# Counting the softmax sums of three groups once, and four projections in halves, in a two-layer graph attention kernel

## The chip, the cores and the metric

The kernel runs on one core of a Trainium2 chip. The metric is the device time of one execution in microseconds (us); lower is better. The core has five engines that run side by side, each through its own list of instructions in order: TensorE (PE; PEld is its weight load) multiplies matrices, VectorE (DVE) and ScalarE (ACT) work elementwise and may read the matmul results in PSUM, GpSimd (POOL) works elementwise on SBUF and issues one kind of DMA, SyncE (SP) issues the other DMAs. Engines wait for each other by semaphores.

## What is computed

16 images, each with 1024 nodes of 256 features and its own 1024 x 1024 adjacency matrix. Two layers follow each other; each normalizes, applies a relu, and adds masked multi-head attention to its input. Layer 0 has 4 heads of 64 features, layer 1 has 8 heads of 32 and biases on q, k and v.

```python
h = jnp.maximum(_layernorm(x, axis=-1), 0.0)
q, k, v = heads(h @ Wq), heads(h @ Wk), heads(h @ Wv)          # per layer
scores = jnp.einsum('bhnd,bhmd->bhnm', q, k) / math.sqrt(D)
scores = jnp.where(adjacency > 0, scores, -jnp.inf)
w = jax.nn.softmax(scores, axis=-1)
out = jnp.einsum('bhnm,bhmd->bhnd', w, v)
x = x + concat(out) @ Wo + bo
```

All of it is in float32. The softmax is computed without a running maximum: exponentials p, the products p v, and the sums of p over the keys (the "counts"), by which the products are divided at the end.

## The kernel before

**Steps.** The attention of an image in a layer is cut into halves of 512 queries (`qh`), each half into two groups (`g`): in layer 1 a group is 4 heads, in layer 0 it is 2. A step of layer 1 handles one tile of 128 keys for the 4 heads of its group, a step of layer 0 two tiles of keys for 2 heads, so each step makes 4 blocks of 128 keys x 512 queries. A group has 8 steps in layer 1 and 4 in layer 0; an image has 32 and 16. The steps of all images stand in one list: layer 0 of image b+2 follows layer 1 of image b, so that each image's layer 1 is framed by layer 0 of others. In what follows c is the first step of an image's layer 1. Its groups 0 to 3 (`2*qh+g`) start at c, c+8, c+16 and c+24, and layer 0 of another image starts at c+32.

**One step on the engines.** `scores` (L501) makes the 4 blocks in two PSUM pairs; `exponentials` masks them on VectorE (L524, two instructions) and takes the exponential on ScalarE (L530); `weigh` (L542) multiplies by v. `weigh` of a step runs two steps later (`LEAD = 2`). There are three PSUM pairs (`ps_s`, 2 banks each), and two single banks: `po` for the weighed sums and `pz` for the counts. The exponentials of an even step lie in a tile of the ring `p0` (7 buffers), those of an odd step in `p10` and `p11` (2 buffers each), so an odd step writes where the odd step four before it was.

**Counts in layer 1** (`count_steps`, L643 to L690). After an odd step's `weigh`, GpSimd adds the odd step's tile to the even one's (L659, two additions). So a group has four sums of pairs, after j = 1, 3, 5 and 7. An accumulating DMA that GpSimd issues (`accumulate`, L643, 1 MB) adds one of them to another. What is left is summed over the 128 keys by `count` (L387): a matmul with a column of ones into the bank `pz`. In groups 0, 1 and 2 the first two sums are joined and counted, and so are the last two: two counts to a group, given in halves of 256 columns at two steps (`halves`) or whole. In group 3 all four are joined by three DMAs and counted once. Image 14 (`brief`) does group 3 otherwise, and the last image (`pairs`) counts every sum of a pair.

**After a group** (`end_group`). `spread` copies the counts from PSUM and sends them by DMA (L420) into a shape in which `invert` takes the reciprocal (L428) and writes it to DRAM (L430); `fetch` reads it back over all partitions (L439); `normalize` multiplies on GpSimd (L447); `end_half` multiplies by Wo (L483) and adds to x. Each is given a number of steps after the group's end.

**The order around it.** `Stream.run` walks over the steps, two at a time in layer 0. In each it issues scores, the weighs that wait, counts that are due, exponentials, and then all that was put down for the step with `later(i, f)`; functions named in `LARGE` go last. If an even step of layer 1 has a LARGE function, its weighs are put off to the next step. Every engine's instructions run in the order of this program. Projections of coming images (`kq`, L304, and `values`, L345: 8 or 16 instructions, 3.63 us or 3.65 us of TensorE) are LARGE and use a PSUM pair; they are put down, like the layer norms (`stats`, `norm`), the transposes by DMA (`turn_blocks`, `put_blocks`, `place_blocks`) and the loads of masks, at fixed steps from c, or from a, the first step of the layer 0 that follows.

Of the kernel before, what the change touches and what calls it, by code (L numbers as in the profile page):

```python
# [10 lines left out]
F32 = mybir.dt.float32  # L11
# [7 lines left out]
P = 128  # L19
# [5 lines left out]
LARGE = ("k", "q", "values", "end_half")  # L25
# [65 lines left out]
def fast_program(ctx, tc, a, w, loads, chk):  # L91
# [89 lines left out]
    class Inputs:  # L181
# [106 lines left out]

        def kq(self, half, is_q):
            if half == 0 and not is_q:  # L290
                self.kT = actp.tile([P, 2, N], F32, tag="kT", name=f"kT_{self.n}")
                self.v = actp.tile([P, NT, E], F32, tag="v", name=f"v_{self.n}")
# [41 lines left out]

        def k(self, half):
            self.kq(half, False)
# [18 lines left out]
    class Group:  # L355


        def __init__(self, inp, mask, qh, g, half):
# [11 lines left out]
            self.waits = ((5, 5), (7, 7), (7, 6), None)[2 * qh + g]  # L370
# [197 lines left out]
    class Stream:  # L568
# [76 lines left out]
        def count_steps(self, i, st):  # L645
# [7 lines left out]
            elif j % 2:  # L653
                one = self.steps[i - LEAD - 1].p
                if gr.last and not (gr.brief or gr.pairs) and j == 7:
                    self.accumulate(gr.two, gr.one)
# [9 lines left out]
                elif j == 3:  # L666
                    self.accumulate(one, gr.one)
                    gr.one = one
                    if not gr.last:
                        self.halves(i + gr.waits[0], gr, one, True, False)  # L670
                    if gr.brief:
                        self.later(i + 6, gr.count, one, True, False)
                elif gr.brief and j == 5:
                    self.halves(i + 5, gr, one, False, False)
                elif gr.brief:
                    self.later(i + 4, gr.count, one, False, st.last)
                elif j == 5:
                    gr.two = one
                elif not gr.last:
                    self.accumulate(one, gr.two)  # L680
                    if gr.qh:
                        self.later(i + 6, gr.count, one, False, True)
                    else:
                        self.halves(i + gr.waits[1], gr, one, False, True)
                else:
                    self.later(i + 1, self.accumulate, one, gr.two)
                    self.later(i + 4, gr.count, one, True, True)
# [12 lines left out]
        def end_group(self, i, gr):  # L700
# [6 lines left out]
            if gr.layer == 0:  # L707
# [5 lines left out]
                at = (3, 4, 5, 7, 11) if gr.qh else (3, 5, 6, 7, 11)  # L713
                if gr.inp.b == B - 1 and gr.qh:
                    at = 3, 4, 5, 7, 13
                if gr.inp.b == 0:
                    at = (2, 3, 4, 5, 8) if gr.qh else (3, 5, 6, 7, 9)
            else:
                at = ((6, 12, 15, 19), (8, 12, 14, 17, 19), (6, 9, 11, 14), None)[2 * gr.qh + gr.g]
# [428 lines left out]
```

## Time and profile before

| what | value |
| --- | --- |
| median of 3 runs | 3096.69 us (3095.47 to 3098.55) |
| profiled execution | 3095.46 us |
| its span, first to last instruction | 3093.7 us |
| granted TensorE clock | 0.999 |
| L387 counts on TensorE | 1928 instructions, 179.7 us |
| L659 additions on GpSimd | 510 of 2429 ns |
| L643 accumulating DMAs | 133 of 1024 KB, issue 919 ns, median 7.7 us to landing |
| L524 on VectorE | 1536 of 1214 ns, 1792.0 us |
| L530 on ScalarE | 1536 of 1055 ns, 1607.8 us |

An f32 matmul of 512 columns stands in the trace as two instructions; four matmuls of 32 rows or columns run beside each other in the array, so a tile of layer 1 is 8 instructions. A matmul's end is modelled, and durations of neighbours overlap: what one costs is read from its start to the next one's start. In lines of a timeline the columns are start, duration, engine, line of the program, operation, out<-in, shapes and number of instructions, and in brackets how long the engine had been idle and who ended that. "PE po L542" in such a bracket is a guess from the semaphores and may be another.

### The profile page before, as it was taken

Reading aid. Unit: us, or ns where it says so; the run is one execution under the profiler, and the core shown is the slowest. Engines: PE = TensorE matmul, PEld = TensorE weight load, DVE = VectorE, ACT = ScalarE, POOL = GpSimd, SP = SyncE. Lnnn points to the kernel's source line nnn. Section 1 sums busy time; section 2 is a strip of 40 time slices with the busy share of each in tenths; the row PEclk is TensorE's granted clock in tenths of the full one; section 3 lists DMA queues with packets and bytes.
Section 4 is the critical chain, followed back from the end, with each engine's and each line's share of the span. In section 5 each row is a group of like instructions: output and inputs, shape, how many; then the busy total and the mean of one; then the engine's idle time right before and its main releaser. Section 6 shows DMA issues by size and latency. Waiting matters only on the chain.

```text
span 3093.7 us, 47320 instructions
## 1 busy us (share of the span) xinstructions
PE 3072.4 (99%) x17398; PEld 1219.0 (39%) x17398; DVE 2473.7 (80%) x2698; ACT 2230.8 (72%) x2436; POOL 2434.0 (79%) x1554
## 2 busy tenths in 40 slices
PE   9999999999999999999999999999999999999998
PEld 4443433434334343443433434343343433434333
DVE  6678787887878888788887887878788787887777
ACT  5667767777777777777777777777777777776675
POOL 3578788787887878878788787887878788787887
PEclk9999999999999999999999999999999999999999
DMA  4225545354463544535445363554535545453331
GB/s 133 62 66 118 126 110 125 115 113 120 103 143 108 120 122 102 141 103 121 119 100 138 106 129 104 114 130 107 127 114 113 127 110 120 120 113 86 76 77 33
DMA packets 259232, 341.40 MB, mean 110 GB/s; under 512 B 58288, under 2 KB 218288, under 8 KB 241968
## 3 DMA queue, kind: packets, MB, share of 16 engines
q0 software_dynamic: 19152, 139.47, 22.6%
q1 hardware_dynamic: 239520, 198.56, 22.3%
q8 instruction: 139, 2.28, 0.3%
q14 instruction: 101, 0.83, 0.1%
q10 hardware_dynamic: 320, 0.26, 0.0%
HBM read 149.95 MB, written 47.96 MB: 64 GB/s over the span
## 4 chain that ended last, share of the span: by engine, by line
PE 93%; DVE 2%; DMA 1%; SPq 1%; ACT 1%; issue 1%; POOL 0%; DVEq 0%; ACTq 0%; POOLq 0%
PE ps L501 31%; PE po L542 29%; PE pq L304 15%; PE pv L345 7%; PE py L483 7%; PE pz L387 4%; DVE p L524 2%; DMA sums<-s 1%; SPq L152 0%; SPq L420 0%; ACT p L530 0%; POOL p L659 0%; DMA p<-p 0%; DMA inv<-vd 0%; DVE x L488 0%
## 5 line engine op out<-in xcount | busy, mean ns | idle before, releaser
L524 DVE SCALAR_TENSOR_TENSOR p<-mask,ps 128x1024 f32<-128x1024 fp8e5 x1536 | 1792.0, 1214 | 360.5 <-PE ps L501 340.5
L530 ACT ACTIVATE p<-p 128x1024 f32<-128x1024 f32 x1536 | 1607.8, 1055 | 633.3 <-DVE p L524 576.5
L659 POOL TENSOR_TENSOR p<-p,p 128x1024 f32<-128x1024 f32 x510 | 1212.6, 2429 | 163.5 <-PE po L542 163.5
L501 PE MATMUL ps<-qT,kT 32*128 32x512 f32 (+1 forms) x6144 | 1074.3, 629 | 5.0 <-DVE p L524 4.2
L542 PE MATMUL po<-p,v 128*32 128x512 f32 (+1 forms) x6144 | 980.3, 600 | 1.6 <-ACT cat L399 1.3
L501 PEld LDWEIGHTS ps<-qT,kT 32*128 32x128 f32 (+1 forms) x6144 | 348.9, 184 | 590.4 <-issue 239.3
L542 PEld LDWEIGHTS po<-p,v 128*32 128x32 f32 (+1 forms) x6144 | 234.2, 118 | 680.9 <-issue 474.5
L555 POOL TENSOR_TENSOR p<-p 128x1024 f32<-128x1024 f32 x128 | 302.5, 2363 | 92.8 <-DVE p L554 87.5
L554 POOL TENSOR_TENSOR p<-p,p 128x1024 f32<-128x1024 f32 x64 | 150.7, 2355 | 170.1 <-DVE p L551 128.7
L345 PE MATMUL pv<-wv,hT 128*128 128x256 f32 x1024 | 237.8, 385 | 0.1
L304 PE MATMUL pq<-hT,wk 128*128 128x512 f32 x512 | 236.7, 605 | 0.7 <-DVE p L524 0.6
L304 PE MATMUL pq<-hT,wq 128*128 128x512 f32 x512 | 236.8, 605 | 0.1
L483 PE MATMUL py<-wo,cat 128*128 128x256 f32 x1008 | 234.4, 386 | 0.1
L447 POOL TENSOR_TENSOR cat<-cat,inv 128x512 f32<-128x512 f32 x127 | 173.8, 1374 | 76.4 <-DMA inv<-vd 75.8
L345 PEld LDWEIGHTS pv<-wv,hT 128*128 128x128 f32 x1024 | 189.4, 190 | 72.6 <-DVE p L524 22.2
L483 PEld LDWEIGHTS py<-wo,cat 128*128 128x128 f32 x1008 | 186.3, 190 | 74.2 <-issue 27.2
L387 PE MATMUL pz<-p,ones 128*32 128x256 f32 (+1 forms) x1928 | 179.7, 444 | 1.3 <-DMA p<-p 1.3
L551 DVE TENSOR_TENSOR p<-p 128x1024 f32<-128x1024 f32 x128 | 178.5, 1394 | 0.0
L643 POOL DMA_DIRECT2D p<-p x133 | 122.2, 919 | 61.2 <-POOL p L659 30.1
L221 ACT ACTIVATE hn<-x,shift,rstd 128x256 f32<-128x256 f32 x251 | 135.6, 588 | 40.3 <-DMA turned<-hn 26.0
L399 ACT COPY cat<-po 128x512 f32<-128x512 f32 x128 | 73.3, 572 | 118.6 <-PE py L483 96.7
L488 DVE TENSOR_TENSOR x<-py,x 128x1024 f32<-128x1024 f32 x63 | 77.1, 1224 | 101.8 <-PE py L483 101.4
(62 smaller groups left out, 1770.3 us busy)
## 6 DMA issues: line engine op xcount, KB each, us to landing
p<-p POOLq DMA_DIRECT2D x133, 1024.0 KB, 7.7
adj<-in_adj_dram SPq DMA_DIRECT2D x512, 128.0 KB, 3.0
turned<-hn SPq DMA_DIRECT2D x58, 512.0 KB, 3.8
hT<-turned SPq DMA_DIRECT2D x232, 128.0 KB, 2.9
x<-in_x_dram SPq DMA_DIRECT2D x128, 128.0 KB, 3.1
inv<-vd SPq DMA_DIRECT2D x128, 128.0 KB, 3.0
inv<-vd SPq DMA_DIRECT2D x252, 64.0 KB, 3.2
out_dram<-x SPq DMA_DIRECT2D x124, 128.0 KB, 2.2
```

Source lines behind the costliest of these rows:

```text
L304: nc.tensor.matmul(pq[:, m, :], wt[self.layer][:, c, ts(m, P)], self.hT[half][:, c, :], start=(c == 0), stop=(c == 1),)
L345: nc.tensor.matmul(pv[:, i, :], self.hT[half][:, c, ts(i, P)], w.v[self.layer][:, c, :], start=(c == 0), stop=(c == 1),)
L387: nc.tensor.matmul(self.s[ts(r, 32), q], w.ones.to_broadcast([P, 32]), of[:, q], start=start and not part, stop=stop and part != 0,)
L447: nc.gpsimd.tensor_mul(o, o, inv)
L483: nc.tensor.matmul(py[:, i, :], self.half.cat[:, c, ts(i, P)], w.o[self.layer][:, c, :], start=(c == 0), stop=(c == 1),)
L501: nc.tensor.matmul(st.ps[i // 2][:, i % 2, :], gr.inp.kT[r * D : (r + 1) * D, gr.g, ts(kt, P)], gr.inp.qT[gr.qh][r * D : (r + 1) * D, gr.g ...
L524: nc.vector.scalar_tensor_tensor(out=half, in0=gr.mask.m[gr.qh][:, kt // 4, :, kt % 4].unsqueeze(1).to_broadcast([P, 2, 512]), scalar=-EDG ...
L530: nc.scalar.activation(half, half, AF.Exp, scale=gr.scale)
L542: nc.tensor.matmul(gr.o[r * D : (r + 1) * D, :], gr.inp.v[:, kt, h * D : (h + 1) * D], st.halves[i // 2][:, i % 2, :], start=(kt == 0), st ...
L551: nc.vector.tensor_add(a, a, b)
L555: nc.gpsimd.tensor_add(a, a, b)
L659: nc.gpsimd.tensor_add(half, half, of)
```

## The change

Seven things are changed, all in when and how often work is issued; what is computed stays the same.

1. Groups 0, 1 and 2 of layer 1 join all four sums by three DMAs, as group 3 did, and count once: group 0 whole at c+18, group 1 in two halves (c+24, c+25), group 2 whole at c+33, which is layer 0's second step.
2. The second accumulation of a group stands behind the additions of j = 7. The third is put down one step later in groups 1 and 3, two steps later in groups 0 and 2, and in image 14 two steps later in all of 0 to 2.
3. Four projections of the next layer 0 (k of the first half at c+8 and c+10, q of the first half at c+12 and c+16, k of the second half at c+20 and c+22, values of the second half at c+28 and c+30) are made in two parts each, each part in the single bank `pz` in place of a PSUM pair. The parts are LARGE.
4. `spread`, `invert`, `fetch` and `normalize` of groups 0 and 2 move: group 0 from (6, 12, 15, 19) to (9, 11, 13, 19) after its end, group 2 from (6, 9, 11, 14) to (10, 12, 14, 16).
5. In the second half of layer 0 `normalize` moves from 7 to 11 steps after the end and `end_half` from 11 to 13 (steps c+12 and c+14 of the layer 1 that runs then).
6. The layer norms of the image whose layer 1 comes next start earlier: for its first half from a-20, a-16, a-15, a-13 to a-26, a-22, a-19, a-17 (c+6, c+10, c+13, c+15), and the DMA transposes with them.
7. Images 14 and 15 get numbers of their own for some of these.

The core of the diff:

```diff
+        def part(self, half, is_q, m):
...
+            pq = ps_o.tile([P, 512], F32, tag="pz", name=f"pq_{self.n}_{half}_{int(is_q)}_{m}")
+            for c in range(2):
+                nc.tensor.matmul(
+                    pq, wt[self.layer][:, c, ts(m, P)], self.hT[half][:, c, :],
+                    start=(c == 0), stop=(c == 1),
+                )
+            (nc.vector.tensor_copy if is_q else nc.scalar.copy)(to[:, m, :], pq)
...
+        def values_part(self, half, m):
+            pv = ps_o.tile([P, 512], F32, tag="pz", name=f"pv_{self.n}_{half}_{m}")
...
-            self.waits = ((5, 5), (7, 7), (7, 6), None)[2 * qh + g]
+            self.waits = (9, 7, 8, 4)[2 * qh + g]
...
-                if gr.last and not (gr.brief or gr.pairs) and j == 7:
-                    self.accumulate(gr.two, gr.one)
                 for k, of in enumerate(st.halves):
                     half = one[:, ts(k, 2), :]
                     nc.gpsimd.tensor_add(half, half, of)
...
+                elif j == 5:
+                    gr.two = one
+                elif st.last and gr.last:
+                    self.accumulate(gr.two, gr.one)
+                    self.later(i + 1, self.accumulate, one, gr.two)
+                    self.later(i + gr.waits, gr.count, one, True, True)
+                elif st.last:
+                    self.accumulate(gr.two, gr.one)
+                    late = not gr.g or gr.qh or gr.inp.b == B - 2
+                    self.later(i + (2 if late else 1), self.accumulate, one, gr.two)
+                    if gr.g:
+                        self.halves(i + gr.waits, gr, one, True, True)
+                    else:
+                        self.later(i + gr.waits, gr.count, one, True, True)
+                else:
                     self.accumulate(one, gr.one)
                     gr.one = one
...
-                at = (3, 4, 5, 7, 11) if gr.qh else (3, 5, 6, 7, 11)
+                at = (3, 4, 5, 11, 13) if gr.qh else (3, 5, 6, 7, 11)
...
-                at = ((6, 12, 15, 19), (8, 12, 14, 17, 19), (6, 9, 11, 14), None)[2 * gr.qh + gr.g]
+                at = ((9, 11, 13, 19), (8, 12, 14, 17, 19), (10, 12, 14, 16), None)[2 * gr.qh + gr.g]
...
-            norms(mine, 0, a - 20, a - 16, a - 15, a - 13, bias=a)
-            block_inputs(mine, 0, a - 10, a - 8, a - 4, a, a + 2, a + 8)
-            norms(mine, 1, a - 14, a - 10, a - 8, a - 6, bias=a + 6)
+            norms(mine, 0, a - 26, a - 22, a - 19, a - 17, bias=a)
+            block_inputs(mine, 0, a - 14, a - 11, a - 5, a, a + 2, a + 8)
+            norms(mine, 1, a - 14, a - 13, a - 8, a - 6, bias=a + 6)
...
-                block_inputs(other, 0, c, c + 1, c + 2, c + 8, c + 16, c + 18)
+                block_inputs(other, 0, c, c + 1, c + 2, (c + 8, c + 10), (c + 12, c + 16), c + 18)
...
-                block_inputs(other, 1, c + 7, c + 8, c + 12, c + 22, c + 26, c + 30)
+                block_inputs(other, 1, c + 7, c + 8, c + 12, (c + 20, c + 22), c + 26, (c + 28, c + 30))
```

The index i in `count_steps` is the step whose turn it is when the weigh of step c+7 (or c+15, c+23) has been issued, that is two steps after it: i = c+9, c+17, c+25.

## The prediction

> **What bounds the kernel now.** I read the page first (busy shares, chain of waits), then the busy time of the stages of one image, then the timelines of TensorE, of GpSimd and of all engines.
>
> ```profile
> PE 3072.4 (99%) x17398; PEld 1219.0 (39%) x17398; DVE 2473.7 (80%) x2698; ACT 2230.8 (72%) x2436; POOL 2434.0 (79%) x1554
> ...
> PE 93%; DVE 2%; DMA 1%; SPq 1%; ACT 1%; issue 1%; POOL 0%; DVEq 0%; ACTq 0%; POOLq 0%
> ```
>
> TensorE sets the time: 99% busy and 93% of the chain. An average hides stages, so here are the two stages of one image in the middle: 16 steps of layer 0, then 32 steps of layer 1 (columns: PE, PEld, DVE, ACT, POOL, clock, DMA).
>
> ```profile
> 1259.98:1336.74 76.76, 76.62 (x340) 31.34 (x336) 59.24 (x64) 56.28 (x60) 58.99 (x41) 1.00 0.50 124
> 1336.74:1449.86 113.12, 113.08 (x738) 43.34 (x736) 95.67 (x105) 82.72 (x94) 94.39 (x57) 1.00 0.47 113
> ```
>
> TensorE is full in both. In layer 1, where the change lies, VectorE has 95.7 and GpSimd 94.4 of 113.1 us: about 85% each, with little room.
>
> **TensorE's prices**, from start to next start in its timeline:
>
> ```profile
> 1380.29 1.14 PE L501 MATMUL ps<-qT,kT 32*128 32x512 f32 x8
> 1381.36 1.06 PE L542 MATMUL po<-p,v 128*32 128x512 f32 x8
> 1382.24 0.61 PE L387 MATMUL pz<-p,ones 128*32 128x256 f32 x8
> 1382.79 1.15 PE L501 MATMUL ps<-qT,kT 32*128 32x512 f32 x8
> 1383.94 3.72 PE L483 MATMUL py<-wo,cat 128*128 128x256 f32 x16
> 1387.59 1.14 PE L501 MATMUL ps<-qT,kT 32*128 32x512 f32 x8
> 1388.66 1.93 PE L542 MATMUL po<-p,v 128*32 128x512 f32 x16
> 1390.52 1.14 PE L501 MATMUL ps<-qT,kT 32*128 32x512 f32 x8
> ```
>
> Scores of a step 1.07 us (1.15 ahead of a full-array product); weighing 0.88 for one step, 1.86 for two in a run; half a count 0.55 at the end of a run; a full-array product 3.65. So a tile of 512 columns costs 0.885 and the end of a run 0.09; half a count inside a run is 0.445. A whole count alone takes 0.98 (1259.01 to 1259.98).
>
> **What is removed.** c is the first layer-1 step of an image. Group 0 loses two whole counts in halves and gets one whole one, group 1 goes from four halves to two, group 2 from two halves and a whole one to one whole one: three tiles, 3 x 0.885 = 2.66 us an image, in images 0 to 14 (the last image counts in pairs and stays). 15 x 2.66 = 39.9 us. Bounds by the rows: 0.445 to 0.98 for a tile.
>
> **Projections in halves.** A half is four of eight instructions, 3.63/2 = 1.82 us (bounds 1.8 to 1.9). Four more even steps become "large": each costs 0.08 (1.15 for 1.07) and joins two weighs into one run (-0.09). Sum: nothing. Their copies are ACT 0.57 x 2 for 1.0 (L399, L349) and DVE 0.69 x 2 for 1.23 (L310, L313), some 0.15 us more each, under ACT's 27% idle time; each bank is needed again two steps (5 us) later. Without that cover they would cost 0.6 us an image.
>
> **What is added on GpSimd.** Each of groups 0 to 2 gets a third accumulating DMA. The issue takes 0.9 us of GpSimd, three are 2.7 of the 18.7 us that it has free in layer 1. The landing is what counts: the third reads what the second writes, so GpSimd must wait for it, in order.
>
> ```profile
> 1402.57 4.70 POOL L659 TENSOR_TENSOR p<-p,p 128x1024 f32<-128x1024 f32 x2 [0.25 <-PE po L542]
> 1407.57 0.90 POOL L643 DMA_DIRECT2D p<-p  x1 [0.30 <-POOL p L659]
> 1410.22 9.38 POOL L659 TENSOR_TENSOR p<-p,p 128x1024 f32<-128x1024 f32 x4 [1.76 <-PE po L542]
> ...
> 1447.22 0.89 POOL L643 DMA_DIRECT2D p<-p  x1 [0.97 <-PE ps L501]
> 1448.36 4.71 POOL L659 TENSOR_TENSOR p<-p,p 128x1024 f32<-128x1024 f32 x2 [0.24 <-PE po L542]
> 1455.30 0.89 POOL L643 DMA_DIRECT2D p<-p  x1 [2.23 <-DMA p<-p]
> ```
>
> The last three lines are group 3 today: the first DMA goes out at 1447.22 and lands 7.54 us later, at 1454.76; GpSimd has finished its additions at 1453.07, stands idle 2.23 us, and issues the dependent DMA 0.54 after the landing. All 133 land in 6.8 to 11.8 us, median 7.7. The first three lines are group 1's last additions (steps c+14, c+15) and DMA today, with nothing dependent behind it.
>
> *Step c+18 (group 1).* The new code puts group 1's third accumulation one step after the second, ahead of the additions of step c+17, and no other GpSimd work lies between. Zero is the start of TensorE's weighs in step c+17; additions start 1.2 later (1409.01 to 1410.22). GpSimd: additions 1.2 to 5.9; second DMA 6.2; landing 13.7 (7.5); third DMA 14.2; free 14.85; additions of c+17 until 17.2 (first half) and 19.55. Behind them are queued the statistics of c+19 (1.6, as at 1359.14), the additions of c+19 to 25.85, a DMA 0.9, the additions of c+21 to 31.45. TensorE unhindered, by the prices: c+18 scores, count, values until 7.56; weighs of c+16/c+17 from 8.63, so the additions of c+17 could have run at 9.85: 5 us late. Who waits: the odd steps' tiles have two buffers, so VectorE's L524 of step c+21 writes where c+17's tile was, and its PSUM pair frees for TensorE's next scores. Today the slack is small: these additions end at 1412.6 and 1414.9, L524 of c+21 starts at 1414.61 and 1415.8. The additions of c+21 gate L524 of c+25 in the same way: 31.45, plus 1.2, plus 0.15 for the semaphore gives 32.8; q of step c+26 needs that pair and would have started at 28.45. TensorE loses 4.4 us. Bounds: 0 (all absorbed) to 5.0 (the whole delay). I take 4.4, since the mechanism stands in the trace, in image 14:
>
> ```profile
> 2904.40 4.83 DVE L524 SCALAR_TENSOR_TENSOR p<-mask,ps 128x1024 f32<-128x1024 fp8e5 x4 [0.94 <-POOL p L659]
> 2905.31 7.31 POOL L659 TENSOR_TENSOR p<-p,p 128x1024 f32<-128x1024 f32 x3
> 2905.68 2.26 PE L501 MATMUL ps<-qT,kT 32*128 32x512 f32 x8
> ```
>
> VectorE waits 0.94 for GpSimd, and scores that take 1.14 take 2.26.
>
> A rule against this reading: the Trainium skill ("DMA: Bandwidth & Descriptors", section "Anatomy of one DMA — SWDGE (gpsimd) path") gives a DMA from GpSimd 2.0 us plus its bytes at 436 GB/s, an estimate of 4.4 us for 1 MB, where the rows here have 7.7. By 4.4 us the third DMA would leave at 11.1, this term would be 1.3 and the whole sum about 3103. The measured landing decides.
>
> *Step c+14 (layer 0's end_half).* The normalizing of layer 0's second half moves from c+8 to c+12, its end_half only from c+12 to c+14. Zero at the weighs of c+9: additions 1.2 to 5.9, second DMA of group 0 at 6.2 (landing 6.8: 13.0), statistics moved to c+10 until 8.4, additions of c+9 until 13.1, third DMA 13.55 (i + 2 in group 0, hence almost no pause), two normalizing products 2.5 us (1374.11) until 16.7. TensorE reaches end_half at 1.86 + 2.97 + 2.93 + 2.97 + 2.93 + 1.15 = 14.8. It waits 1.9; bounds 0 and 2.5; I take 1.9.
>
> *Groups 2 and 3.* Group 2's third DMA follows a step with additions: a pause of at most 1 us, with over 2 us of slack before L524 of c+31. Reckoned on from the same zero, it lands at about 52 and its count comes at about 57. Group 3's second DMA behind the additions takes away the idle 2.23; TensorE's count at c+37 is unaffected, since the chain there was not GpSimd's: nothing. The third then lands some 1 to 2 us ahead of its count.
>
> *SyncE.* Moved sums, fetches and puts keep two or more steps to their users; SyncE is idle for up to 20 us between them in layer 1 (1378.48 to 1398.20). Group 2's chain in c+35 to c+41 is spaced as group 3's is today. Nothing; uncovered, one DMA's 3 us.
>
> *Image 14's layer 1* (2856 to 2971): TensorE isn't full there and GpSimd is (32.85 of 35 us from 2900). Saving 2.7 shows only in part, three DMAs add 2.7 and pauses of up to 2.4 each. Bounds -2.7 and +10; I take +2.
>
> **Sum.** 14 images x (4.4 + 1.9 - 2.66) = +51; image 14 +2; together +53 us. The span 3093.7 becomes 3147, the profiled execution (3095.46, 1.8 around the span) 3148; the median shown is 1.2 above it. Forecast 3149 us.
>
> **Rivals.**
> A, only c+18 costs; normalizing comes in time because the additions start earlier than I draw them. 14 x (4.4 - 2.66) + 2 = +26: 3123. For it: 1.9 us is small. Against: the same landing stands in both.
> B, faster: the buffers absorb the pause. Place: L524 of c+21 to c+25. Decides if the additions of c+17 come no more than about 1.5 us late, that is with a landing below about 4 us or without a wait on it. 3096.7 - 39.9 = 3057. For it: TensorE has all that is needed in time today. Against: the idle 2.23 at 1455.30.
> C, the saved tiles return as waits for VectorE (95.7 of then 110.5 us): no change, 3097; against it, 13% of VectorE stays free.
> The change doing less than it says, a count kept or a tile waiting for its landing at c+24: third landing 21.7, count 24.2, so no.
>
> **How the numbers follow.** Forecast case 0.45 (own range 3128 to 3168), A 0.22, B 0.28 (3050 to 3075), C 0.05. The range 3055 to 3165 cuts some 0.1 off each end. 0.2% is 6 us, about what these runs can tell from no change. Faster 0.28 (B), same 0.05 (C), slower 0.67.
>
> **What would show it.** L387 falls from 1928 instructions by 56 an image (24 + 16 + 16) to 1088, its busy time by about 40 us. L643 x178. GpSimd idle some 6 us ahead of one L643 an image, L524 ended by "POOL p L659" for several us an image; "POOL cat L447" ending TensorE's wait before L483. If the idle time before L643 is there but L524 never waits for L659, B is right and the two-buffer argument is wrong.

## The result and the profile after

The changed kernel takes 3174.14 us (median; 3171.27 to 3176.5), the one before 3096.74 beside it: ratio 1.0249, interval 1.0231 to 1.0267. It is slower by 2.5%, more than the range held. Its profiled span is 3169.4 us, 75.7 above before. Line numbers moved: scores L501 are now L539, masking L524 is L562, weighing L542 is L580, the accumulating DMA L643 is L681, the additions L659 are L695, end_half L483 is L521, counts L387 are L425, normalize L447 is L485; the half projections are L348.

From the page after: the busy line, the chain's shares, and the groups of the accumulating DMA and of end_half (busy, mean ns | idle before them and who ended most of it).

```profile
PE 3094.0 (98%) x16558; PEld 1203.7 (38%) x16558; DVE 2477.1 (78%) x2712; ACT 2239.1 (71%) x2478; POOL 2476.5 (78%) x1599
...
PE 64%; POOL 16%; DMA 7%; issue 6%; DVE 4%; ACT 2%; SPq 1%; POOLq 0%; DVEq 0%; ACTq 0%
...
L681 POOL DMA_DIRECT2D p<-p x178 | 165.0, 927 | 182.4 <-DMA p<-p 118.3
...
L521 PE MATMUL py<-wo,cat 128*128 128x256 f32 x1008 | 239.5, 389 | 16.6 <-POOL cat L485 14.1
```

TensorE has 840 instructions less, as reckoned, and yet it no longer sets the end alone: its share of the chain fell from 93% to 64%, and GpSimd and the DMAs have 23%. GpSimd stands idle ahead of the group L681 for 182 us in all (61 before, ahead of L643): 118.3 by the brackets, and some 150 by the times, are waits that a landing ends; 17 more are its own additions ending.

The two stages of the image shown before, one of layer 0 and one of layer 1 (columns: PE, PEld, DVE, ACT, POOL, clock, DMA):

```profile
1285.41:1364.30 78.89, 78.15 (x348) 31.36 (x344) 60.88 (x65) 56.94 (x61) 63.00 (x43) 1.00 0.53 131
1364.30:1480.94 116.64, 112.91 (x674) 42.09 (x672) 93.66 (x105) 82.17 (x95) 93.52 (x58) 0.99 0.56 128
```

Layer 1 went from 113.12 to 116.64, and TensorE, which had 113.08 of work there, stands idle for 3.7 us; its clock is 0.99. Layer 0, where the prediction saw no loss, went from 76.76 to 78.89. Over all images the layer 1 stages are 50.2 us longer (4.6 of it in the last one, of images 14 and 15) and the layer 0 stages 25.6.

**The pause.** GpSimd's timeline in that layer 1 (c is 1364.30):

```profile
1434.41 0.85 POOL L681 DMA_DIRECT2D p<-p  x1
1443.50 0.85 POOL L681 DMA_DIRECT2D p<-p  x1 [8.24 <-PE ps L539]
1444.06 4.98 POOL L695 TENSOR_TENSOR p<-p,p 128x1024 f32<-128x1024 f32 x2
```

The second and third DMA of group 1 are 9.1 us apart. The bracket names TensorE, but it is the landing: the same half microsecond lies behind it as at 1455.30 before, so the second one landed at 1442.96, 8.55 us after its issue. The additions of c+17 start at 1444.06. VectorE shows who waits for them, and TensorE for VectorE:

```profile
1446.78 1.22 DVE L562 SCALAR_TENSOR_TENSOR p<-mask,ps 128x1024 f32<-128x1024 fp8e5 x1 [2.84 <-POOL p L695]
1449.08 3.48 DVE L562 SCALAR_TENSOR_TENSOR p<-mask,ps 128x1024 f32<-128x1024 fp8e5 x3 [1.08 <-POOL p L695]
```

```profile
1440.10 1.98 PE L348 MATMUL pq<-hT,wk 128*128 128x512 f32 x4
1442.02 1.22 PE L539 MATMUL ps<-qT,kT 32*128 32x512 f32 x8
...
1445.02 1.13 PE L539 MATMUL ps<-qT,kT 32*128 32x512 f32 x4
1448.05 1.13 PE L539 MATMUL ps<-qT,kT 32*128 32x512 f32 x4 [1.91 <-DVE p L562]
1449.11 3.31 PE L348 MATMUL pq<-hT,wk 128*128 128x512 f32 x4
...
1462.55 3.70 PE L307 MATMUL pq<-hT,wq 128*128 128x512 f32 x8 [0.81 <-DVE p L562]
```

In all, L562 waits for L695 in 92 places, 110.2 us where it was 5 places and 5.3. q of c+26 starts 34.0 us after the weighs of c+17 (1428.54); the prediction said 32.85, unhindered 28.45 (28.4 before, on average). One line doesn't fit: half a projection of k, four instructions, takes 3.31 us, where the other half took 1.98 two steps earlier. The granted clock says why, in windows of 2 us (columns as above, the clock is the third number from the end):

```profile
1446.00:1448.00 2.00, 0.15 (x2) 0.00 (x0) 1.22 (x1) 0.00 (x0) 2.00 (x2) 1.00 0.96 199
1448.00:1450.00 2.00, 1.95 (x6) 0.93 (x7) 0.92 (x1) 1.06 (x1) 2.00 (x4) 0.91 1.23 291
1450.00:1452.00 2.00, 2.00 (x3) 0.34 (x1) 2.00 (x3) 1.59 (x2) 1.92 (x3) 0.50 0.78 233
1452.00:1454.00 2.00, 2.00 (x13) 0.67 (x16) 0.64 (x2) 1.93 (x3) 2.00 (x2) 0.74 0.18 65
```

A microsecond after TensorE's wait of 1.91 its clock falls to 0.5, for 3.4 us in all: 1.7 us lost on top of the wait.

**Ends of the other two steps.** TensorE at c+14, waiting for normalize (L485), and at the start of the next layer 0; then VectorE there, GpSimd ahead of it, and TensorE at the same start in the kernel before:

```profile
1417.11 0.70 PE L521 MATMUL py<-wo,cat 128*128 128x256 f32 x2 [0.48 <-POOL cat L485]
1418.34 3.29 PE L521 MATMUL py<-wo,cat 128*128 128x256 f32 x14 [0.53 <-POOL cat L485]
...
1480.94 1.99 PE L539 MATMUL ps<-qT,kT 64*128 64x512 f32 x8
1483.53 2.26 PE L539 MATMUL ps<-qT,kT 64*128 64x512 f32 x8 [0.60 <-DVE p L562]
```

```profile
1479.93 1.22 DVE L562 SCALAR_TENSOR_TENSOR p<-mask,ps 128x1024 f32<-128x1024 fp8e5 x1 [1.03 <-POOL p L695]
1482.25 4.81 DVE L562 SCALAR_TENSOR_TENSOR p<-mask,ps 128x1024 f32<-128x1024 fp8e5 x4 [1.10 <-POOL p L695]
```

```profile
1475.39 0.87 POOL L681 DMA_DIRECT2D p<-p  x1 [2.22 <-DMA hT<-turned]
```

```profile
1449.86 3.70 PE L501 MATMUL ps<-qT,kT 64*128 64x512 f32 x16
```

This step belongs to group 2: its second DMA went out at 1465.54 and lands 9.31 us later, GpSimd issues the third one after 2.22 us of idle time, and VectorE waits for the additions behind it. The scores of layer 0's first steps take 4.78 us to the next start, where they took 3.64.

### The profile page after: what moved, and what is told of

It is laid out like the page before. It is cut to its first block, busy times and chain, and to the rows that moved or that the text cites. A ratio compares the mean times of both kernels' runs of the same rounds, so it can differ in the third digit from the quotient of the medians.

```text
span 3169.4 us, 45804 instructions
## 1 busy us (share of the span) xinstructions
PE 3094.0 (98%) x16558; PEld 1203.7 (38%) x16558; DVE 2477.1 (78%) x2712; ACT 2239.1 (71%) x2478; POOL 2476.5 (78%) x1599
## 4 chain that ended last, share of the span: by engine, by line
PE 64%; POOL 16%; DMA 7%; issue 6%; DVE 4%; ACT 2%; SPq 1%; POOLq 0%; DVEq 0%; ACTq 0%
PE ps L539 20%; PE po L580 20%; POOL p L695 12%; PE pq L307 7%; PE py L521 7%; DMA p<-p 5%; PE pv L383 4%; DVE p L562 3%; PE pq L348 3%; POOL cat L485 2%; PE pz L425 2%; DMA hT<-turned 1%; SPq L458 1%; POOL p L681 1%; POOL rstd L211 0%
## 5 line engine op out<-in xcount | busy, mean ns | idle before, releaser
L562 DVE SCALAR_TENSOR_TENSOR p<-mask,ps 128x1024 f32<-128x1024 fp8e5 x1536 | 1795.5, 1215 | 411.2 <-PE ps L539 276.4
L695 POOL TENSOR_TENSOR p<-p,p 128x1024 f32<-128x1024 f32 x510 | 1223.0, 2503 | 118.3 <-PE po L580 118.3
L539 PE MATMUL ps<-qT,kT 32*128 32x512 f32 (+1 forms) x6144 | 1116.7, 632 | 32.6 <-DVE p L562 29.4
L580 PE MATMUL po<-p,v 128*32 128x512 f32 (+1 forms) x6144 | 967.1, 599 | 1.3 <-ACT cat L437 1.3
L539 PEld LDWEIGHTS ps<-qT,kT 32*128 32x128 f32 (+1 forms) x6144 | 358.1, 184 | 692.1 <-DVE p L562 327.0
L580 PEld LDWEIGHTS po<-p,v 128*32 128x32 f32 (+1 forms) x6144 | 239.4, 118 | 671.0 <-issue 491.5
L681 POOL DMA_DIRECT2D p<-p x178 | 165.0, 927 | 182.4 <-DMA p<-p 118.3
L485 POOL TENSOR_TENSOR cat<-cat,inv 128x512 f32<-128x512 f32 x127 | 191.6, 1552 | 113.1 <-DMA inv<-vd 113.0
L521 PE MATMUL py<-wo,cat 128*128 128x256 f32 x1008 | 239.5, 389 | 16.6 <-POOL cat L485 14.1
L592 POOL TENSOR_TENSOR p<-p,p 128x1024 f32<-128x1024 f32 x64 | 155.2, 2425 | 124.6 <-DVE p L589 84.3
L521 PEld LDWEIGHTS py<-wo,cat 128*128 128x128 f32 x1008 | 186.2, 191 | 96.4 <-issue 35.1
L307 PE MATMUL pq<-hT,wq 128*128 128x512 f32 x400 | 184.8, 605 | 12.7 <-DVE p L562 12.7
L383 PE MATMUL pv<-wv,hT 128*128 128x256 f32 x800 | 185.7, 385 | 0.0
L167 ACT ACTIVATE mask<-adj,numbers 128x1024 fp8e5<-128x1024 int32 x128 | 145.8, 1139 | 40.4 <-DMA adj<-in_adj_dram 40.3
L383 PEld LDWEIGHTS pv<-wv,hT 128*128 128x128 f32 x800 | 148.0, 190 | 57.1 <-issue 25.2
L230 POOL TENSOR_TENSOR x<-x,bo 128x1024 f32<-128x1024 f32 x64 | 160.1, 2642 | 0.0
L595 POOL TENSOR_TENSOR p<-p,p 128x1024 f32<-128x1024 f32 x64 | 151.6, 2369 | 5.0
```

Source lines behind the costliest of these rows:

```text
L307: nc.tensor.matmul(pq[:, m, :], wt[self.layer][:, c, ts(m, P)], self.hT[half][:, c, :], start=(c == 0), stop=(c == 1),)
L383: nc.tensor.matmul(pv[:, i, :], self.hT[half][:, c, ts(i, P)], w.v[self.layer][:, c, :], start=(c == 0), stop=(c == 1),)
L485: nc.gpsimd.tensor_mul(o, o, inv)
L521: nc.tensor.matmul(py[:, i, :], self.half.cat[:, c, ts(i, P)], w.o[self.layer][:, c, :], start=(c == 0), stop=(c == 1),)
L539: nc.tensor.matmul(st.ps[i // 2][:, i % 2, :], gr.inp.kT[r * D : (r + 1) * D, gr.g, ts(kt, P)], gr.inp.qT[gr.qh][r * D : (r + 1) * D, gr.g ...
L562: nc.vector.scalar_tensor_tensor(out=half, in0=gr.mask.m[gr.qh][:, kt // 4, :, kt % 4].unsqueeze(1).to_broadcast([P, 2, 512]), scalar=-EDG ...
```

## The experiments

Edits are to the changed kernel (3174) if nothing else is said; the kernel before took 3095 to 3096 beside each. "Clock loss" is the span times what the mean granted clock lacks to 1: 4 us before (0.9987), 22 in the changed kernel (0.993).

**The pause at c+18, and normalizing, each alone.** `e1_late`: the third accumulation two steps later in group 1 too.

```diff
-                    late = not gr.g or gr.qh or gr.inp.b == B - 2
+                    late = True
```

> Group 1's third accumulation goes out two steps after the second, as in groups 0 and 2, in place of one. Theory (GpSimd stands still for the second one's landing, some 8 us, and the additions behind it are late): the pause ahead of the third DMA of group 1 shrinks below 2 us, layer 1 takes some 4 to 5.5 us less an image in 13 images, so about 3174 - 60 = 3115 us (3100 to 3130). Rival 1 (the projections in halves cost the time): no change, 3174. Rival 2 (more DMA traffic slows everything): no change, 3174.

Measured 3112.43 (1.0051, 1.0035 to 1.0068). The pause was worth 61.7 us, as the theory said.

`e2_norm`: normalize and end_half back at 7 and 11 steps.

```diff
-                at = (3, 4, 5, 11, 13) if gr.qh else (3, 5, 6, 7, 11)
+                at = (3, 4, 5, 7, 11) if gr.qh else (3, 5, 6, 7, 11)
```

> Layer 0's second-half normalizing and end_half go back to 7 and 11 steps. Theory: TensorE's wait of some 1.3 us for the normalized products at c+14 goes, 14 x 1.3 = 18 us less, 3156 (3150 to 3165); the pause at c+18 stays as it is. Rivals 1 and 2: no change, 3174.

Measured 3158.73 (1.0204, 1.0187 to 1.0221): worth 15.4. `f1_late_norm` makes both edits.

> Both mends together: group 1's third accumulation two steps after the second, and layer 0's normalizing and end_half at 7 and 11. Theory: the two costs add, 3112 - 16 = 3096 (3088 to 3104), the same as before; layer 1 then stands some 2.5 us an image under before, layer 0 still some 2 over. Rival (the costs are one backlog, so that mending one already takes most of it): 3110.

Measured 3099.97 (1.0014, 1.0004 to 1.0023). The two costs nearly add (74 us for 61.7 and 15.4). Its layer 1 stages are 21.7 us shorter than before in all, its layer 0 stages 28.9 longer. Of the image shown, in the order of the stages above:

```profile
1255.07:1334.12 79.05, 78.22 (x349) 31.35 (x345) 60.81 (x65) 56.95 (x61) 63.16 (x43) 1.00 0.53 131
1334.12:1444.95 110.83, 110.56 (x675) 41.80 (x673) 93.05 (x105) 82.14 (x95) 93.19 (x58) 1.00 0.59 135
```

Group 2's count moved from layer 1 to layer 0, so layer 1 has four tiles of counts less and layer 0 one more. In images 0 to 13 that should be 49.6 us less and 12.4 more; it is 29.1 less and 28.9 more, together 0.2 less than before. So 20.5 us are missing in layer 1 and 16.5 in layer 0, with neither of the two waits left.

`f4_first`: the second accumulation ahead of the additions again.

```diff
                 one = self.steps[i - LEAD - 1].p
+                if st.last and not (gr.brief or gr.pairs):
+                    self.accumulate(gr.two, gr.one)
...
                 elif st.last:
-                    self.accumulate(gr.two, gr.one)
```

> The second accumulation goes back ahead of the additions of the last odd step, in all four groups; everything else as changed. Theory: it then lands under the additions (4.7 us), GpSimd's idle time ahead of group 1's third DMA falls from 8.2 to some 3.5 us, and layer 1 takes 3 to 4.5 us less an image: 3174 - 50 = 3124 (3110 to 3140); group 3 gets back its 2 us wait, which TensorE does not feel. Rival (the order of the second accumulation does not matter, or helps as changed): 3174 or more.

Measured 3112.49 (1.0044, 1.0027 to 1.0061), as much as by e1_late. By the brackets GpSimd still waits 98.3 us for landings (118.3 in the changed kernel), but 3.9 at the longest and not 8.7, for 4.7 us of additions now lie between issue and need.

**Is it the landing that the third accumulation waits for?** `e3_free` and `f3_late_free` let it read the joined sum of the first two pairs, which nobody is writing; the third pair's sum is missing from their counts. f3_late_free has the edit of e1_late besides.

```diff
-                    self.later(i + (2 if late else 1), self.accumulate, one, gr.two)
+                    self.later(i + (2 if late else 1), self.accumulate, one, gr.one)
```

> The third accumulation of groups 0 to 2 reads the sum of the first two pairs, which is long complete, in place of the tile that the second one writes; the third pairs' sum (j = 4, 5) is left out of the counts, everything else is issued as before, the same number of DMAs of the same size. Theory: with no landing to wait for, the idle time ahead of L681 goes from 182 us to under 60, L562's waits for L695 nearly vanish, and the time falls by 14 x (5.5 + 1.0) = 90 us to about 3083 (3065 to 3100). Rival 2 (traffic, issue cost): no change, 3174. Rival 1 (halves): no change.

Measured 3171.91 (1.0248, 1.0231 to 1.0266): nothing gained, a clear miss. The pause was gone, but the place where TensorE stops was not. GpSimd, VectorE and TensorE at that place (c is 1363.53):

```profile
1433.51 1.77 POOL L681 DMA_DIRECT2D p<-p  x2
1437.51 4.70 POOL L695 TENSOR_TENSOR p<-p,p 128x1024 f32<-128x1024 f32 x2 [2.23 <-PE po L580]
```

```profile
1447.00 0.25 DVE L466 RECIPROCAL vn<-sums 128x16 f32<-128x16 f32 x1 [4.68 <-DMA sums<-s]
```

```profile
1444.15 1.13 PE L539 MATMUL ps<-qT,kT 32*128 32x512 f32 x4
1448.39 1.13 PE L539 MATMUL ps<-qT,kT 32*128 32x512 f32 x4 [3.11 <-DVE p L562]
1449.45 3.45 PE L348 MATMUL pq<-hT,wk 128*128 128x512 f32 x4
```

Two accumulating DMAs go out together and are in flight at once; they land 8.6 and 13.0 us after their issues. The small DMAs that carry group 0's counts to `invert`, 2 KB each, land 7.6 to 9.0 us after theirs; the median of all such DMAs in this run is 1.9. VectorE's reciprocal stands ahead of L562 in its list and waits 4.68. One wait has taken the place of another, longer than the one removed (3.11 for 1.91), and the clock falls after it in every image: clock loss 39 us (0.988).

> As e1_late, but the third accumulation of groups 0 to 2 reads the sum of the first two pairs (the third pairs' sum is left out of the counts), so it has no landing to wait for, and it is never in flight at the same time as the second for long. In e3_free the pause was gone but VectorE then waited 4.7 us for the DMA of the sums. Theory (that wait came from two 1 MB DMAs in flight together): it is gone here, and against e1_late only group 2's landing wait goes, 3112 - 17 = 3095 (3088 to 3104). Rival (the sums' DMA is late for another reason, as the count at c+18): the wait stays, 3112 or more.

Measured 3093.51 (0.9992, 0.9983 to 1.0002). With two steps between the two DMAs the reciprocal waits as usual, and the dependence on landings is worth some 19 us more after e1_late.

`g1_ring3` gives the odd steps' tiles three buffers, and the even ones six in place of seven, for space; `g4_p0six` has only the second half of that.

```diff
-                pp.tile([P, 2, 512], F32, tag=f"p1{i}", bufs=2, name=f"p_{st.n}_{i}") for i in range(2)
+                pp.tile([P, 2, 512], F32, tag=f"p1{i}", bufs=3, name=f"p_{st.n}_{i}") for i in range(2)
...
-            st.p = pp.tile([P, 4, 512], F32, tag="p0", bufs=7, name=f"p_{st.n}")
+            st.p = pp.tile([P, 4, 512], F32, tag="p0", bufs=6, name=f"p_{st.n}")
```

> The changed kernel with three buffers in place of two for the odd steps' tiles, and six in place of seven for the even steps' (for room in SBUF); order and DMAs as changed. Theory (a late addition on GpSimd costs time because VectorE needs the tile of four steps before): with three buffers VectorE needs the tile of six steps before, some 6 us later, so GpSimd's pause of 8 us before group 1's third DMA stays in the trace, but L562's waits for L695 (110 us) fall below 20 and the time by 14 x (5.5 + 1) = 90 us, to about 3085 (3070 to 3105); TensorE's 1.3 us at c+14 stays. Rival (the additions are late but TensorE is held by something else, the counts or the landing itself): no change, 3174.

> Control for g1_ring3: only the six buffers for the even steps' tiles. Theory: each tile's last reader is some steps ahead of its reuse, so no change, 3174 (3168 to 3185).

Measured 3183.46 (1.0293, 1.0280 to 1.0307) and 3178.95 (1.0275, 1.0260 to 1.0290). In time a miss; in the trace the argument of the two buffers holds. GpSimd's pause is still there in g1_ring3 (8.25 us ahead of 1444.18), but L562 waits for L695 in 2 places and 0.6 us in all, and q of c+26 starts 28.6 us after the weighs of c+17 (1457.80 and 1429.21), against 28.45 unhindered. Then comes this, in TensorE's and VectorE's timelines:

```profile
1457.80 3.70 PE L307 MATMUL pq<-hT,wq 128*128 128x512 f32 x8
1464.60 3.21 PE L539 MATMUL ps<-qT,kT 32*128 32x512 f32 x8 [3.10 <-DVE p L562]
```

```profile
1463.33 2.35 DVE L562 SCALAR_TENSOR_TENSOR p<-mask,ps 128x1024 f32<-128x1024 fp8e5 x2 [5.58 <-DMA p<-p]
```

VectorE waits 5.58 us for the next accumulating DMA (issued 1456.31, late by the pause) to have read or written a tile that the ring of six wants again; such waits come to 91.5 us, and the clock loss to 43. The late GpSimd is paid one way or the other. g4_p0six shows that the smaller ring alone costs little.

**The halves.** `e4_whole` makes the four projections whole again.

```diff
-                block_inputs(other, 0, c, c + 1, c + 2, (c + 8, c + 10), (c + 12, c + 16), c + 18)
+                block_inputs(other, 0, c, c + 1, c + 2, c + 8, c + 16, c + 18)
...
-                block_inputs(other, 1, c + 7, c + 8, c + 12, (c + 20, c + 22), c + 26, (c + 28, c + 30))
+                block_inputs(other, 1, c + 7, c + 8, c + 12, c + 22, c + 26, c + 30)
```

> The four projections whole again, in PSUM pairs, at c+8, c+16, c+22 and c+30; all else as changed. Theory (GpSimd's pause): the same within 10 us, 3165 to 3185. Rival 1 (halves cost the time): back by most of the loss, below 3130.

Measured 3267.37 (1.0549, 1.0531 to 1.0566), 93 us more: a miss of both. TensorE at c+14 and at c+22 of one image (c is 1405.98):

```profile
1460.33 0.70 PE L521 MATMUL py<-wo,cat 128*128 128x256 f32 x2 [1.81 <-POOL cat L485]
1461.55 4.89 PE L521 MATMUL py<-wo,cat 128*128 128x256 f32 x14 [0.53 <-POOL cat L485]
...
1494.60 1.18 PE L539 MATMUL ps<-qT,kT 32*128 32x512 f32 x4 [2.77 <-DVE p L562]
1496.89 6.40 PE L307 MATMUL pq<-hT,wk 128*128 128x512 f32 x8 [1.12 <-DVE p L562]
```

The same two waits as in the changed kernel, longer (1.81 for 0.48; 2.77 and 1.12 for 1.91), and after both the clock falls: 4.89 us where 3.29 were shown above, 6.40 for 3.70. Clock loss 66 us (0.980), 44 of the 93. My reading, not tried by itself: with no half projection at c+10 and c+12 TensorE gets to end_half earlier and waits there; at c+22 a whole projection wants one of the three PSUM pairs that the late VectorE holds, which a half in `pz` doesn't.

**Does the wait bring the clock down?** In 17 of the traces (all but g5_before_ring3 and the two that follow), from 25 to 3040 us, each stretch in which TensorE stood idle for over 0.7 us at full clock is set beside the granted clock up to 4 us behind it. Below 1.0 us: down in 2 of 59; 1.0 to 1.5: 28 of 75, of which 12 directly follow a longer wait; 1.5 to 1.9: 22 of 25; 1.9 to 2.7: 26 of 32; longer: 38 of 38. It then stands at 0.5 for 3.4 or 6.8 us, but for two cases of more. To test it, `i1_free_fill` (on e3_free, its counts as told there) and `i2_fill` (on the changed kernel) give TensorE work that nobody needs, just ahead of the scores of c+22, where it waits.

```diff
+        def fill(self, half):
+            pq = ps_o.tile([P, 512], F32, tag="pz", name=f"pf_{self.n}_{half}")
+            for c in range(3):
+                nc.tensor.matmul(
+                    pq, w.k[self.layer][:, c % 2, :P], self.hT[half][:, c % 2, :],
+                    start=(c == 0), stop=(c == 2),
+                )
...
+            later(c + 21, other.fill, 1)
```

> e3_free (its third accumulation reads the first pair's sum again, so the third pairs' sum is missing from the counts), with three full-array matmuls of 512 columns (2.75 us by 3.65 for four) put into TensorE's list ahead of the scores of c+22; nobody reads their result. In e3_free TensorE waits there 2.3 to 3.5 us in every image, and after it the granted clock stands at 0.5 for 3.4 or 6.8 us, 34 us lost ahead of the last stage. Theory (the wait itself brings the clock down, and that, not the wait alone, is what e3_free lost): TensorE has work in the wait, the clock stays at 1.00 in most images, and the kernel becomes faster by the work added: 3172 - 34 + 2 = 3140, 3132 to 3150. Rival (the clock falls for another reason, or the clock in the records doesn't set the time): 3165 or more, up to 3210 if the 14 x 2.75 us add.

Measured 3130.32 (1.0113, 1.0098 to 1.0129), just under the range: 41.6 us faster than e3_free, with 14 x 2.75 us of work more. Mean clock 0.999, and TensorE at c+21 and c+22:

```profile
1433.42 2.84 PE L357 MATMUL pf<-hT,wk 128*128 128x512 f32 x6
1436.19 1.69 PE L547 MATMUL ps<-qT,kT 32*128 32x512 f32 x8
1437.81 1.98 PE L348 MATMUL pq<-hT,wk 128*128 128x512 f32 x4
```

The wait is filled, the half projection takes 1.98 and not 3.45, and the clock is down in none of images 0 to 13. So it was the wait that brought the clock down, and the clock that cost the time.

> The changed kernel with two such matmuls (1.83 us) ahead of the scores of c+22. There 6 of 14 images have the clock at half after this wait, 13.7 us lost. Theory: those 13.7 go, and the added work lies in the wait for GpSimd's late additions (4.5 us an image by now, at c+22 and c+26): 3174 - 13 = 3161, 3154 to 3168. Rival (the matmuls add to the time): 3175 to 3200.

Measured 3180.02 (1.0274, 1.0260 to 1.0288): a miss. Where the work was put, the theory held: the clock stays at 1.00 there, and from the scores of c+18 to those of c+26 all but one image take 28.3 us, where they took 28.3 to 34.0, 21 us less in all. But 19.5 come back at c+14, in six images, by a new wait for normalize. GpSimd and TensorE there:

```profile
1613.59 0.90 POOL L689 DMA_DIRECT2D p<-p  x1 [2.11 <-DMA p<-p]
1614.24 2.79 POOL L493 TENSOR_TENSOR cat<-cat,inv 128x512 f32<-128x512 f32 x2
```

```profile
1615.86 0.70 PE L529 MATMUL py<-wo,cat 128*128 128x256 f32 x2 [2.59 <-POOL cat L493]
```

Group 0's second DMA (1604.30) lands after 9.0 us there and delays the third one and normalize behind it; in the changed kernel the third went out 7.2 us after the second with no wait. Why that landing is longer stays open.

**Group 2 and layer 0.** `f2_far`: f1_late_norm with group 2's third accumulation four steps late and its count two steps later, image 14 left out.

> As f1_late_norm, and group 2's third accumulation four steps after the second, its count at c+35. Theory (what layer 0 loses at its start is the lateness from group 2's landing): L562's waits of 1.1 us for L695 at layer 0's start go, 14 x 1.2 = 17 us less than f1_late_norm, 3079 (3070 to 3088). Rival (layer 0 loses it to group 3's own landing wait of 1.9 us or to the loads): no change from f1_late_norm.

Measured 3103.32 (1.0022, 1.0012 to 1.0031): a miss. L562's waits for L695 fall from 47.8 to 16.5 us, but ScalarE waits 54.8 us for the adjacency (39.6 in f1_late_norm), and TensorE for its copies of k behind them (8.0 us, 2.7 there). That the later accumulation slows these loads was not tried by itself. `h5_two_old`: f1_late_norm with group 2 counted twice as before (values of c+28 and c+30 whole).

```diff
+            self.twice = bool(qh) and not self.last
...
+                elif gr.twice and j == 3:
+                    self.accumulate(one, gr.one)
+                    self.halves(i + gr.waits[0], gr, one, True, False)
...
+                elif gr.twice:
+                    self.accumulate(one, gr.two)
```

> Third accumulation two steps later everywhere, normalizing at 7 and 11, and group 2 counts twice as it did before, all in layer 1 (its values projection of c+28 and c+30 is whole at c+30, since the bank of the counts is taken then). Theory (layer 0's loss comes from group 2's third accumulation, whose landing and whose late additions reach into layer 0): the layer 0 stages, +28.9 us in all with group 2 counted once, come back to within 5 us of before; the layer 1 stages rise from -21.7 by 14 x 0.885 = 12.4 and fall by 2 in image 14; time 3100 - 29 + 12 - 2 = 3081, 3077 to 3088. Rival (layer 0 loses by the earlier layer norms and their transposes, which stay): layer 0 stays at +16 or more, time 3097 to 3112.

Measured 3090.59 (0.9983, 0.9974 to 0.9992). The layer 0 stages are 2.2 us above before, from 28.9. The layer norms are still moved here, so layer 0's excess came with counting group 2 once: 12.4 of it is the tile that moved there, the rest is what goes with it (the third accumulation, the later chain from spread to normalize, the values in halves). Which of these it is stays open, since f2_far took the waits for the additions away and layer 0 gained nothing. The time is 10 above what I gave since my sum put one tile back into layer 1 and there are two (24.8 us, not 12.4; the images' stages show 24.3). So images 0 to 13 are only 2.4 us faster than in f1_late_norm: what layer 0 gets back, layer 1 pays for in tiles. Most of the gain, 10.1 us, is in the last stage, where image 14 too counts group 2 twice. The layer 0 stage that follows the layer 1 shown of before, 76.34 there and 79.36 in the changed kernel:

```profile
1448.12:1524.52 76.40, 76.40 (x341) 31.35 (x337) 59.19 (x64) 56.28 (x60) 59.00 (x41) 1.00 0.51 125
```

**Towards a better version.** `g2_best` is f1_late_norm with groups 0 and 1 issuing the second accumulation ahead of the additions; `g3_ring3_best` has the buffers of g1_ring3 too; `h4_image14` besides counts image 14's groups 0 to 2 twice as before, and `h6_both_old` group 2 of all images. `g5_before_ring3` is the kernel before with the buffers of g1_ring3.

> f1_late_norm with the second accumulation of groups 0 and 1 ahead of the additions (it lands under them), groups 2 and 3 behind them. Theory: the remaining landing waits of groups 0 and 1 go, 0.5 us an image: 3100 - 7 = 3093 (3086 to 3100). Rival: the two pauses were hidden already, 3100.

> g2_best with three buffers for the odd steps' tiles and six for the even ones. Theory: TensorE is full again and keeps most of the 2.66 us an image that the counts saved, 3097 - 40 + 5 to 15: 3062 to 3072, faster than both kernels. Rival (VectorE or the loads take over as the bound in layer 1): 3090.

> The best version so far (three buffers for the odd tiles, six for the even ones, third accumulation two steps later, normalizing at 7 and 11, second accumulation of groups 0 and 1 ahead of the additions; 3089.3), with image 14 counting groups 0 to 2 twice as before. Theory (the stage of images 14 and 15 is 8.7 us longer because GpSimd is full there and three DMAs and their landings came in): that stage comes back to within 2 us of before, time 3081, 3078 to 3084. Rival (the stage is longer by the ring of six or by the moved norms): stage still +6 or more, time 3087 to 3091.

> The version before, and group 2 counted twice as before in all images (values of c+28 and c+30 whole at c+30). If both terms add up: 3089.3 - 8.7 (image 14) - 23 (layer 0) + 12.4 (group 2's tile back in layer 1) = 3070, 3066 to 3076. If the two landings that are left hide others behind them: 3080 or more.

> The kernel before the change with three buffers for the odd tiles and six for the even ones. VectorE waits for GpSimd's additions for 5.3 us in the whole trace there, so the larger ring has little to take away. Theory (the ring matters only with the pause): 3092 to 3097. Rival (what is gained in the best version comes from the ring alone): 3089 or less.

Measured: g2_best 3102.52 (1.0025, 1.0015 to 1.0035), no gain, a miss; g3_ring3_best 3089.29 (0.9980, 0.9971 to 0.9989), a miss by 17 us, near the rival's 3090; h4_image14 3076.90 (0.9939, 0.9926 to 0.9953), better than its range; h6_both_old 3092.81 (0.9990, 0.9981 to 0.9999), a miss, where the wrong tile count of h5_two_old is in my sum again and 10 us stay unexplained beyond it; g5_before_ring3 3092.75 (0.9992, 0.9983 to 1.0001), so the larger ring by itself does nothing. h4_image14 is the best one, 0.6% faster than before and 3.1% faster than the changed kernel. It counts group 2 once in images 0 to 13, and these take 11.3 us less than before; with group 2 counted twice (h6_both_old) they take 3.3 more. So with these buffers group 2's single count is no loss. The last stage of h4_image14 (images 14 and 15), and below it that of g3_ring3_best:

```profile
2844.67:3075.45 230.78, 219.33 (x1572) 82.11 (x1570) 175.19 (x175) 160.67 (x171) 188.47 (x114) 0.99 0.28 65
```

```profile
2845.29:3091.50 246.21, 227.23 (x1516) 83.26 (x1514) 175.02 (x175) 160.60 (x171) 191.02 (x117) 0.96 0.33 73
```

With image 14's three groups counted once, and the moves that go with it, this stage is 15.4 us longer in the profiled executions (the medians differ by 12.4), with TensorE idle 7.5 us more and at clock 0.96 for 0.99.

## Why the prediction fell short

The direction was right, and so were the two places of the forecast and the waits that it names there. The size was not: 53 us forecast on the span, 75.7 measured, and several sizes that are wrong on their own cancel in part. For images 0 to 13, from the stages and the starts in the traces:

| term | forecast | measured | from |
| --- | --- | --- | --- |
| counts removed, with the weighs beside them | -37.2 | -39.7 | f1_late_norm |
| projections in halves, with end_half beside them | 0 | +8.2 | f1_late_norm |
| scores held up and idle time, layer 1 | 0 | +14.3 | f1_late_norm |
| the same in layer 0 | 0 | +16.9 | f1_late_norm |
| pause at c+18, with the clock behind it | +61.6 | +60.3 | e1_late |
| normalize at c+14 | +26.6 | +13.7 | e2_norm |
| the last two together, less than their sum | not reckoned | -2.5 | f1_late_norm |
| last stage, images 14 and 15 | +2 | +4.6 | the changed kernel |
| sum | +53 | +76 | |

**The step that failed** is the sum's "- 2.66" an image, taken as kept whole while the rest of the image is put at nothing. In f1_late_norm, where neither of the two priced waits is left, 37.2 us should remain as a gain; 0.2 do. Three terms that the prediction put at nothing take it. Of the projections in halves it says "Sum: nothing": a half takes 1.92 us to the next start (1440.10 to 1442.02 above), where 1.82 was reckoned from half of a whole one, within bounds of 1.8 to 1.9; that is 8.2 us. "Group 2's third DMA follows a step with additions: a pause of at most 1 us, with over 2 us of slack": the pause was 2.22 us, and layer 0 loses 13.2 us beyond its tile in the changed kernel and 16.5 in f1_late_norm. h5_two_old shows that this comes with group 2's single count and not with the moved norms, which were put at nothing too. The third is 14.3 us of layer 1 itself: 8.6 in scores that take longer to the next start, 5.8 idle. Its cause stays open.

**The step that is missing** is the clock. Every matmul behind the wait was reckoned at full speed, and 13.7 us are lost by it in 6 of 14 images. From c+18 to c+31 an image takes 47.5 us, and 43.0 without the pause (e1_late), as long as before: 4.5 us, of which the clock has 1.0 and the wait 3.5. So the forecast's 4.4 for the wait alone came out by luck: the wait was smaller, and the clock that was not reckoned made up for it. The trace before had the clock to be seen, in image 14:

```profile
2885.90 1.13 PE L501 MATMUL ps<-qT,kT 32*128 32x512 f32 x4 [0.92 <-DVE p L524]
```

```profile
2889.00:2891.00 2.00, 2.00 (x9) 0.43 (x2) 0.64 (x2) 1.25 (x2) 2.00 (x2) 0.55 1.02 213
```

One idle stretch of 0.92 us is followed by 3.4 us at 0.5. The Trainium skill ("TensorE: Matmul & The Clock Gate", section "HAM oscillation — how this bites in real kernels") warns of TensorE gaps above some 3.4 us; here waits of 1.5 us and more were enough most times, so by that rule this term would have been next to nothing as well, and the runs decide. Its window of 3.4 us ("Part 1: The HAM clock gate") is the length that the traces show.

The landing was priced with the 7.5 us of one row; the DMA in question takes 8.55. c+14 was the right step with too large a size: 1.9 us an image forecast, 1.1 by e2_norm's time (15.4 us). Image 14's +2 lay within its bounds, and h4_image14 shows that the single counts cost that stage more than the page lets one see, since other edits gain there.

The halves have a use that the prediction did not see: without them the changed kernel would be at 3267. They use no PSUM pair.

Rival A, only c+18 costs, falls by e2_norm; rival B, the buffers absorb it, by L562's 110.2 us; "less than it says" falls by the 840 instructions and the 182 us of idle time at L681. C, no change, falls for the changed kernel, but f1_late_norm is what it describes: the saved tiles come back as other waits and as the halves' own cost. L387's busy time fell by 57.9 us, not 40: durations of neighbours overlap, a half stands as 0.61 and costs 0.45 to 0.55. The range ended at 3165, even below the forecast's own 3168, and neither had room for a term that wasn't in the sum.

## What to carry to other kernels

A dependent accumulating DMA costs its engine the whole landing of the one before, so put as much work of the same engine between the two as the landing lasts, and ask what stands behind it in the list. A wait of TensorE is not paid by its length alone: price each one above some 1.5 us with half a clock behind it, and fill it if there is anything to fill it with. Work taken off a full engine is only a gain where the engines next to it can follow: with both pauses mended nothing of the forecast 37.2 us was left, and in the best version, with three buffers for the odd tiles, 11.3 of it in images 0 to 13. And price a piece that is cut in two by a row of the piece, not by half of the whole.

## What the runs showed of the hardware

- TensorE's granted clock falls to 0.5, mostly for 3.4 or 6.8 us, after idle stretches as short as 1.5 to 1.9 us (22 of 25), and in every case here after more than 2.7 (38 of 38).
- Two 1 MB accumulating DMAs in flight at once land after 8.6 and 13.0 us, and 2 KB DMAs issued beside them after 7.6 to 9.0, where the run's median is 1.9 (e3_free).
- In these traces the releaser named in a bracket can be an engine ("PE ps L539") where the wait ends half a microsecond after a landing; in the changed kernel 40 of the 41 waits of over 1 us ahead of an accumulating DMA that a landing precedes end 0.53 or 0.54 us after one.
